# A transformer block on one core: the order of the beginning, before the first scores

## Chip, cores and metric

The kernel runs on one core of one Trainium2 chip. The metric is the device time of one execution in microseconds (us), the median over several runs. Lower is better.

## What is computed

The reference is one transformer block on x of shape 2 x 1024 x 256, with a context of shape 2 x 154 x 192, all in fp32: self-attention with 16 heads of 64, cross-attention to the context, and a gated feed-forward part. Cut to what matters:

```python
def _layernorm(x, g, b, eps=1e-05):
    mu = jnp.mean(x, axis=-1, keepdims=True)
    var = jnp.var(x, axis=-1, keepdims=True)
    return (x - mu) * jax.lax.rsqrt(var + eps) * g + b

h = _layernorm(x, ln1_g, ln1_b)
x = _attention(h, h, sa_wq, sa_wk, sa_wv, sa_wo, sa_bo) + x
h = _layernorm(x, ln2_g, ln2_b)
x = _attention(h, cond_emb, ca_wq, ca_wk, ca_wv, ca_wo, ca_bo) + x
h = _layernorm(x, ln3_g, ln3_b)
p = h @ ff_w1 + ff_b1
a, gate = (p[..., :D_FF], p[..., D_FF:])
h = a * jax.nn.gelu(gate, approximate=False) @ ff_w2 + ff_b2
return h + x
```

The change touches only the first layer norm of the first batch and the first three projection halves that read it.

## The kernel before

The order of all work is written out by hand: `tc.manual_schedule()` keeps every engine's instructions in the order in which the Python code issues them. There are three long loops, one for self-attention, one for cross-attention and one for the feed-forward part. In each step of a loop, some pieces of projections, norms and output products are run beside the attention work. A piece issues its TensorE work and returns a function, the store, which reads the result out of PSUM; `flush(stores)` calls the stores that are waiting.

Ahead of the first loop stands the beginning, which this case is about. Batch 0 of x is 8 tiles of 128 rows. They are loaded in four pairs (tiles 0-1, 2-3, 4-5, 6-7) by `load_x` at L79, pairs 0 and 4 by the queue of SP and pairs 2 and 6 by the queue of ACT (a pair is named by its first tile). The gain and shift of the first norm, the parameter columns `cols`, are loaded by the ACT queue at L94, one element per partition and row of 128, so in pieces of 4 bytes. The first weights and the other parameters follow on the queue of SP (L109, L133, L140, L104).

The norm has four kinds of pieces:

- `stats(t)` for one tile: the statistics `st_ln` (L190) and their aggregate `mv_ln` (L191), both on VectorE (DVE);
- `deviation(t)` for a pair: `var_ln` (L196, on DVE in the beginning) and `rstd_ln` by a power on GpSimd (POOL, L200);
- `normalize(t)` for a pair: the offset `off_ln` (DVE, L206) and two activations to `xn_ln` (ACT, L212);
- `turn(t)` for a pair: four TensorE (PE) transposes into a PSUM tile `ph_ln` (L221), and a store of two copies to `hT_ln`, one for each half c of the 256 features, with gain and shift applied. In the beginning both copies are on DVE (L230), elsewhere on ACT (L234).

`project_half` (L290) multiplies a weight slice with 512 rows of `hT_ln`: two products, for c = 0 and c = 1, of 512 columns each; the record holds two PE entries for each of them. The store is an ACT copy (L297 for keys, L298 for queries). The first half of rows is made of pairs 0 and 2, the second of pairs 4 and 6. The first scores (L370) need the queries of the first half (`q0`) and the keys of both halves (`k0`, `k1`).

Before the pieces, 26 transposes of the identity into an unused PSUM tile are run on PE (`warm`, L866). PSUM tiles come from `mm_tile` and `sum_tile`, pools of two banks each.

Of the kernel before, what the change touches and what calls it, by code (L numbers as in the profile page):

```python
# [13 lines left out]
P = 128  # L14
# [4 lines left out]
def tile_transformer_block(ctx: ExitStack, tc: tile.TileContext, a: dict, out: bass.AP):  # L19
    nc = tc.nc  # L20
    x, cond = a["x"], a["ctx_768"]
    w = {k[len("L0_xattn_"):]: v for k, v in a.items() if k.startswith("L0_xattn_")}
# [11 lines left out]
    NC = D // P  # L34
# [5 lines left out]
    HB = 512  # L40
# [23 lines left out]
    def mm_tile(name):  # L64
        return ps_m.tile([P, HB], F32, tag="mm", name=name)

    def sum_tile(name):

        return ps_o.tile([P, HB], F32, tag="po", name=name)
# [7 lines left out]
    def load_x(queue, b, t):  # L77

        queue.dma_start(  # L79
            out=xt[b, t // GT][:, t % GT:t % GT + 2, :],  # L80
            in_=x[b, t * P:(t + 2) * P, :].rearrange("(t p) d -> p t d", p=P),
        )
# [3 lines left out]
    names = ["ln1_g", "ln1_b", "ln2_g", "ln2_b", "ln3_g", "ln3_b", "ff_b1"]  # L86
    n_rows = sum(w[n].shape[0] // P for n in names)
    cols = const.tile([P, n_rows], F32, tag="cols", name="cols")
    row_of, r = {}, 0
    for n in names:  # L90
        k = w[n].shape[0] // P
        row_of[n] = r
        if n.startswith("ln1"):
            nc.scalar.dma_start(out=cols[:, r:r + k], in_=w[n].rearrange("(r p) -> p r", p=P))  # L94
            n_cols = r + k
        r += k
    rows = pp_.tile([n_rows - n_cols, P], F32, tag="P", name="rows")
    for t in range(0, NT, 2):
        load_x(nc.scalar if t % 4 else nc.sync, 0, t)
    bias = {}  # L100

    def load_bias(n):
# [13 lines left out]
    wsl, wo = {}, {}  # L116
# [14 lines left out]
    for n in names[2:]:  # L131
        k = w[n].shape[0] // P
        nc.sync.dma_start(  # L133
            out=rows[row_of[n] - n_cols:row_of[n] - n_cols + k, :],
            in_=w[n].rearrange("(r p) -> r p", p=P),
# [9 lines left out]
    ident = const.tile([P, P], F32, tag="ident", name="ident")  # L145
# [28 lines left out]
    def norm_pieces(kind, b, first=False):  # L174

        ln = {"sa": "ln1", "ca": "ln2", "ff": "ln3"}[kind]  # L180
        g0, b0 = row_of[ln + "_g"], row_of[ln + "_b"]
        st = {}

        def stats(t):
            if t == 0:
                st["hT"] = hT[kind, b] = p2.tile([P, NC, S], F32, tag="hT", name=f"hT_{ln}_{b}")
            if t % 2 == 0:
                st["mv", t] = small.tile([P, 2, 2], F32, tag="mv", name=f"mv_{ln}_{b}_{t}")
            s6 = small.tile([P, 6], F32, tag="st", name=f"st_{ln}_{b}_{t}")
            nc.vector.bn_stats(s6, xt[b, t // GT][:, t % GT, :])  # L190
            nc.vector.bn_aggr(st["mv", t // 2 * 2][:, t % 2, :], s6)  # L191

        def deviation(t):
            mv = st["mv", t]
            var = small.tile([P, 2], F32, tag="var", name=f"var_{ln}_{b}_{t}")
            (nc.vector if first else nc.gpsimd).tensor_scalar(  # L196
                var, mv[:, :, 1], EPS, 1.0, op0=ALU.add, op1=ALU.mult
            )
            rstd = small.tile([P, 2], F32, tag="rstd", name=f"rstd_{ln}_{b}_{t}")
            nc.gpsimd.tensor_tensor(rstd, var, power, ALU.pow)  # L200
            st["rstd", t] = rstd

        def normalize(t):
            rstd = st["rstd", t]
            off = small.tile([P, 2], F32, tag="off", name=f"off_{ln}_{b}_{t}")
            nc.vector.scalar_tensor_tensor(  # L206
                off, st["mv", t][:, :, 0], -1.0, rstd, op0=ALU.mult, op1=ALU.mult
            )
            pool, tag = (one, "xn") if narrow(kind, b) and not first else (pp_, "P")
            xn = st["xn", t] = pool.tile([P, 2, D], F32, tag=tag, name=f"xn_{ln}_{b}_{t}")  # L210
            for i in range(2):
                nc.scalar.activation(  # L212
                    xn[:, i, :], xt[b, t // GT][:, t % GT + i, :], AF.Identity,
                    bias=off[:, i:i + 1], scale=rstd[:, i:i + 1],
                )

        def turn(t):
            ph = spare["bank"](f"ph_{ln}_{b}_{t}").rearrange("p (c n) -> p c n", c=NC)
            for i in range(2):
                for c in range(NC):  # L220
                    nc.tensor.transpose(  # L221
                        ph[:, c, i * P:(i + 1) * P], st["xn", t][:, i, c * P:(c + 1) * P], ident
                    )

            def store():
                for c in range(NC):
                    own = st["hT"][:, c, t * P:(t + 2) * P]
                    gain, shift = cols[:, g0 + c:g0 + c + 1], cols[:, b0 + c:b0 + c + 1]
                    if first:
                        nc.vector.tensor_scalar(  # L230
                            own, ph[:, c, :], gain, shift, op0=ALU.mult, op1=ALU.add
                        )
                    else:
                        nc.scalar.activation(  # L234
                            own, ph[:, c, :], AF.Identity, bias=shift, scale=gain
                        )

            return store

        return (  # L240
            [lambda t=t: stats(t) for t in range(NT)],
            *([lambda t=t, f=f: f(t) for t in range(0, NT, 2)] for f in (deviation, normalize, turn)),
        )

    def narrow(kind, b):

        return kind == "sa" or kind == "ca" and b < B - 1
# [35 lines left out]
        side.append((False, (), lambda: add_biases(kind, b)))  # L283


    def project_half(dst, name, wt, h, n, mul=None):

        pq = mm_tile(f"p{name}_{n}")
        for c in range(NC):
            nc.tensor.matmul(  # L290
                pq, lhsT=wt[:, c, :], rhs=h[:, c, n * HB:(n + 1) * HB],
                start=(c == 0), stop=(c == NC - 1),
            )
        if mul is None:

            dk = dst.rearrange("p (h n j) -> p n h j", h=2, j=KB)[:, n * NK // 2:(n + 1) * NK // 2]
            return lambda: nc.scalar.copy(dk, pq.rearrange("p (n h j) -> p n h j", h=2, j=KB))  # L297
        return lambda: nc.scalar.activation(dst[:, n * HB:(n + 1) * HB], pq, AF.Copy, scale=mul)  # L298
# [20 lines left out]
    def self_pieces(b, pr):  # L319

        t = {}

        def start():
            t["h"] = hT["sa", b]
            t["q"] = p2.tile([P, S], F32, tag="QT", name=f"q_sa{b}_{pr}")
            t["k"] = p2.tile([P, S], F32, tag="KT", name=f"k_sa{b}_{pr}")
            t["v"] = pt_.tile([P, NT, 2, P], F32, tag="V", name=f"v_sa{b}_{pr}")
            qk["sa", b, pr] = (t["q"], t["k"], t["v"])

        def q(n):  # L330
            if n == 0:
                start()
            return project_half(t["q"], f"q_sa{b}_{pr}", wsl["sa", pr, "q"], t["h"], n, scale)

        def k(n):
            return project_half(t["k"], f"k_sa{b}_{pr}", wsl["sa", pr, "k"], t["h"], n)

        def v(n):
            return project_self_values(t["v"], wsl["sa", pr, "v"], t["h"], b, pr, n)

        return [lambda f=f, n=n: f(n) for f in (q, k, v) for n in range(2)]
# [88 lines left out]
    def run(piece):  # L430
        done = piece()
        if done is not None:
            (adds if getattr(done, "adds", False) else stores).append(done)

    def flush(queue):
        for fn in queue:
            fn()
        queue.clear()
# [142 lines left out]
    def cross_pieces(b, pr):  # L581
# [3 lines left out]
        def q(n):  # L585
            if n == 0:
                t["q"] = p2.tile([P, S], F32, tag="QT", name=f"q_ca{b}_{pr}")
                t["k"] = p2.tile([P, S], F32, tag="KT", name=f"k_ca{b}_{pr}")
                qk["ca", b, pr] = (t["q"], t["k"])
            return project_half(t["q"], f"q_ca{b}_{pr}", wsl["ca", pr, "q"], hT["ca", b], n, scale)  # L590
# [262 lines left out]
    with tc.manual_schedule():  # L853
        stats, deviation, normalize, turn = norm_pieces("sa", 0, True)
# [3 lines left out]
        def emit(*pieces):  # L858
            for piece in pieces:
                run(piece)  # L860
            flush(stores)


        warm = sum_tile("warm")
        for _ in range(26):
            nc.tensor.transpose(warm[:, :P], ident, ident)  # L866
        emit(stats[0], stats[1], deviation[0], stats[2], stats[3], deviation[1])
        emit(normalize[0], stats[4], stats[5], deviation[2])
        emit(normalize[1], turn[0])
        emit(normalize[2], turn[1])  # L870
        emit(stats[6], stats[7], deviation[3], q0, normalize[3], k0)
        emit(turn[2])
        emit(turn[3])
        emit(k1)
        later.append(lambda: load_pair("sa", units[1][1]))
        later.append(lambda: load_pair("sa", units[2][1]))
# [7 lines left out]
        for p in range(SA):  # L884
# [15 lines left out]
            h, hg = divmod(p, SH)  # L900
# [40 lines left out]
        for k in range(FF):  # L941
            c = CA + k
# [56 lines left out]
```

## Time and profile before

| What | Value |
|---|---|
| median of 3 runs | 1179.57 us (1178.59 to 1180.47) |
| the profiled execution, its own time | 1178.48 us |
| its span, first to last instruction | 1176.6 us |
| PE busy over the span | 1143.3 us, 97% |
| start of the first scores (L370) | 22.68 us |

The profile is of one execution. Times in it count from the first instruction, and the execution's own time is 1.9 us longer than its span. "PEclk" is the clock that TensorE was granted, 1.00 being full speed. The view of stages gives, for each stretch of time, each engine's busy time; the chain of waits follows the work back from the last instruction.

### The profile page before, as it was taken

What the parts mean: (1) busy time and instruction counts of PE and PEld (TensorE: products, weight loads), DVE (VectorE), ACT (ScalarE), POOL (GpSimd) and SP (SyncE); (2) the same over time, 40 slices, a digit from 0 to 9 for tenths busy, and PEclk for the clock granted to TensorE, in tenths of its full rate; (3) what the DMA queues carried; (4) which work ended last, traced back from release to release, by engine and by line L of the source; (5) the groups of instructions that cost most, each with busy time, mean ns of one, the idle gap of its engine ahead of it and who ended that gap; (6) DMA issues with size and microseconds to landing.
All of it is one profiled execution on the core that took longest, in us unless ns stands there. A gap on an engine that the chain in (4) does not pass through costs nothing.

```text
span 1176.6 us, 31689 instructions
## 1 busy us (share of the span) xinstructions
PE 1143.3 (97%) x11907; PEld 669.7 (57%) x11907; DVE 830.9 (71%) x1172; ACT 642.9 (55%) x2053; POOL 670.7 (57%) x1563
## 2 busy tenths in 40 slices
PE   7999999999999999999999988999999999999998
PEld 4434445545545545545545433665555567888887
DVE  3888888898888888889999888556655574232222
ACT  3656776666656656656666765456655572041111
POOL 1678777877777777777777777445644453030000
PEclk8999999999999999999999998999999999999999
DMA  2321011011111111111111110176444433000000
GB/s 63 92 61 27 18 27 21 22 33 21 26 25 22 24 25 21 28 22 21 28 23 21 24 21 6 46 173 156 102 107 102 102 80 73 1 19 9 18 10 18
DMA packets 87018, 51.06 MB, mean 43 GB/s; under 512 B 30742, under 2 KB 77650, under 8 KB 86866
## 3 DMA queue, kind: packets, MB, share of 16 engines
q1 hardware_dynamic: 83650, 46.42, 17.4%
q10 hardware_dynamic: 3216, 2.62, 0.7%
q8 instruction: 94, 1.54, 0.6%
q14 instruction: 58, 0.48, 0.1%
HBM read 19.52 MB, written 2.10 MB: 18 GB/s over the span
## 4 chain that ended last, share of the span: by engine, by line
PE 75%; POOL 6%; ACT 6%; DMA 4%; DVE 4%; issue 3%; SPq 2%; ACTq 0%; DVEq 0%; POOLq 0%
PE po L417 14%; PE s L370 13%; PE pa L809 9%; PE py_sa L348 5%; PE py_ca L348 5%; PE pf L832 5%; PE pq_ca L290 4%; ACT p L381 4%; PE poc L721 4%; DMA st<-st 3%; PE pk_sa L290 3%; PE pq_sa L290 3%; PE sc L645 3%; PE pv_sa L305 3%; POOL p L481 3%
## 5 line engine op out<-in xcount | busy, mean ns | idle before, releaser
L381 ACT ACTIVATE p<-s,st 128x512 f32<-128x512 f32 x512 | 345.2, 686 | 219.9 <-DVE st L530 210.4
L481 POOL TENSOR_SCALAR p<-p,rd,ee 128x512 f32<-128x512 f32 x512 | 387.6, 772 | 43.8 <-DVE rd L477 43.2
L530 DVE TENSOR_REDUCE st<-s 128x2 f32<-128x1024 f32 x256 | 301.4, 1219 | 45.9 <-PE s L370 38.1
L495 DVE STREAM_TRANSPOSE pT<-p 128x1024 f32<-128x1024 f32 x256 | 302.4, 1218 | 0.6 <-POOL p L481 0.5
L370 PE MATMUL s<-k_sa,q_sa 64*32 64x512 f32 x4096 | 256.4, 600 | 20.5 <-ACT p L381 19.3
L417 PE MATMUL po<-pT,v_sa 64*64 64x256 f32 x4096 | 236.3, 380 | 1.2 <-DVE pT L495 1.2
L417 PEld LDWEIGHTS po<-pT,v_sa 64*64 64x64 f32 x4096 | 151.0, 133 | 110.5 <-issue 40.4
L672 POOL TENSOR_SCALAR p<-p,rden 128x154 f32<-128x154 f32 x256 | 97.4, 402 | 119.3 <-DVE rden L669 118.1
L370 PEld LDWEIGHTS s<-k_sa,q_sa 64*32 64x32 f32 x4096 | 58.8, 106 | 153.8 <-ACT p L381 67.8
L661 ACT ACTIVATE p<-sc,neg 128x154 f32<-128x154 f32 x256 | 96.0, 394 | 88.6 <-DVE rden L669 84.4
L809 PE MATMUL pa<-hT_ln,wf 128*128 128x256 f32 x512 | 121.0, 379 | 0.0
L818 DVE SCALAR_TENSOR_TENSOR u<-pa,cols,gate 128x256 f32<-128x256 f32 x64 | 31.0, 484 | 124.1 <-ACT gate L815 124.1
L815 ACT ACTIVATE gate<-pa,cols 128x256 f32<-128x256 f32 x64 | 30.3, 474 | 152.1 <-PE pa L809 152.1
L809 PEld LDWEIGHTS pa<-hT_ln,wf 128*128 128x128 f32 x512 | 96.8, 190 | 13.7 <-issue 0.8
L381 ACT ACTIVATION_READ_ACCUMULATOR p<-s,st 128x1 f32 x512 | 103.5, 202 | 0.0
L650 DVE TENSOR_REDUCE neg<-sc 128x6 f32<-128x924 f32 (+1 forms) x48 | 48.6, 1013 | 48.3 <-PE sc L645 48.3
L405 POOL TENSOR_TENSOR zz<-ee,st 128x8 f32<-128x8 f32 x128 | 26.0, 203 | 84.3 <-ACT ee L403 84.3
L305 PEld LDWEIGHTS pv_sa<-sa_wv,hT_ln 128*128 128x128 f32 x512 | 59.3, 192 | 16.3 <-issue 12.9
L832 PE MATMUL pf<-wf,u 128*128 128x256 f32 x256 | 65.0, 379 | 0.2 <-DVE u L818 0.2
L305 PE MATMUL pv_sa<-sa_wv,hT_ln 128*128 128x128 f32 x512 | 62.4, 278 | 0.0
L290 PE MATMUL pq_sa<-hT_ln,sa_wq 128*128 128x512 f32 x128 | 61.2, 621 | 0.6 <-DVE hT_ln L230 0.6
L290 PE MATMUL pk_sa<-hT_ln,sa_wk 128*128 128x512 f32 x128 | 60.7, 610 | 1.2 <-DVE hT_ln L230 1.2
(73 smaller groups left out, 1228.4 us busy)
## 6 DMA issues: line engine op xcount, KB each, us to landing
wf<-pT_ca SPq DMA_DIRECT2D x128, 128.0 KB
st<-st SPq DMA_DIRECT2D x512, 1.0 KB
v_sa<-v_sa SPq DMA_DIRECT2D x64, 128.0 KB
wf<-in_L_xattn_ff_w_dram SPq DMA_DIRECT2D x12, 256.0 KB
sa_wq<-in_L_xattn_sa_wq_dram SPq DMA_DIRECT2D x16, 128.0 KB
sa_wk<-in_L_xattn_sa_wk_dram SPq DMA_DIRECT2D x16, 128.0 KB
sa_wv<-in_L_xattn_sa_wv_dram SPq DMA_DIRECT2D x16, 128.0 KB
ca_wq<-in_L_xattn_ca_wq_dram SPq DMA_DIRECT2D x16, 128.0 KB
```

What stands on the lines that cost most here:

```text
L290: nc.tensor.matmul(pq, lhsT=wt[:, c, :], rhs=h[:, c, n * HB:(n + 1) * HB], start=(c == 0), stop=(c == NC - 1),)
L305: nc.tensor.matmul(pv[:, i * P:(i + 1) * P], lhsT=h[:, c, (n * GT + i) * P:(n * GT + i + 1) * P], rhs=wt[:, c, :], start=(c == 0), stop=(c ...
L348: nc.tensor.matmul(py[:, :D], lhsT=o[:, i, t * P:(t + 1) * P], rhs=wo[kind][:, half * HP + i, :], start=(i == 0), stop=(i == HP - 1),)
L370: nc.tensor.matmul(sc[a4 * KB:(a4 + 1) * KB, j, :], lhsT=q[r, c:c + KB], rhs=k[r, h * HB:(h + 1) * HB], start=True, stop=True, tile_positi ...
L381: nc.scalar.activation(pr[:, j, :], sc[:, j, :], AF.Exp, bias=st[:, 0, 0, i, j:j + 1], accum_out=st[:, 0, 1, i, j:j + 1],)
L417: nc.tensor.matmul(po[a2][j * DH:(j + 1) * DH, :QH // 2], lhsT=v[r, t, e, j * DH:(j + 1) * DH], rhs=pT[r, j * NK + n, :], start=(t == 0 an ...
L481: nc.gpsimd.tensor_scalar(pr[:, j, :], pr[:, j, :], rd[:, c:c + 1], ee[:, 0, c:c + 1], op0=ALU.mult, op1=ALU.mult,)
L495: nc.vector.transpose(halves[h][:, :, c:c + KB], groups.pop(0).rearrange("p j (n k) -> p (j n) k", k=KB))
L530: nc.vector.tensor_reduce(st[:, 0, 0, i, :], sc[i], AX.X, ALU.max, negate=True)
L672: nc.gpsimd.tensor_scalar(pr_[:, j, i, :T], pr_[:, j, i, :T], rden[:, j, i:i + 1], 1.0, op0=ALU.mult, op1=ALU.mult,)
L809: nc.tensor.matmul(pa[:, half, :TF * P], lhsT=w1[:, c, half * DF + f * P:half * DF + (f + 1) * P], rhs=h[:, c, t0 * P:(t0 + TF) * P], star ...
L832: nc.tensor.matmul(sums[blk][i][:, :D], lhsT=sums[blk, "u"][:, f, i * P:(i + 1) * P], rhs=w2[:, f, :], start=(f == 0), stop=(f == NF - 1),)
```

## The change

Five edits, all in the beginning:

1. The two loads of `cols` are issued behind the loads of x on the ACT queue, not ahead of them.
2. The pieces are emitted in another order: `deviation` and `normalize` of pair 0 come earlier among the statistics, `turn(4)` stands between `q0` and `k0` on PE, and `turn(6)` between `k0` and `k1`. Before, both stood behind `k0`.
3. The copies of pairs 2 and 6 are shared: c = 0 stays on DVE and c = 1 goes to ACT.
4. The identity transposes become 46: 32 at the start, 10 behind the transposes of pair 0 and 4 behind those of pair 2. They use a tile of the other PSUM pool.
5. `k1` is computed in two parts of 256 columns, so that the first part needs only pair 4.

```diff
         row_of[n] = r
         if n.startswith("ln1"):
-            nc.scalar.dma_start(out=cols[:, r:r + k], in_=w[n].rearrange("(r p) -> p r", p=P))
             n_cols = r + k
         r += k
     rows = pp_.tile([n_rows - n_cols, P], F32, tag="P", name="rows")
     for t in range(0, NT, 2):
         load_x(nc.scalar if t % 4 else nc.sync, 0, t)
+    for n in names[:2]:
+        k = w[n].shape[0] // P
+        nc.scalar.dma_start(
+            out=cols[:, row_of[n]:row_of[n] + k], in_=w[n].rearrange("(r p) -> p r", p=P)
+        )
...
-                    if first:
+                    if first and (c == 0 or t % 4 == 0):
                         nc.vector.tensor_scalar(
                             own, ph[:, c, :], gain, shift, op0=ALU.mult, op1=ALU.add
                         )
...
-    def project_half(dst, name, wt, h, n, mul=None):
+    def project_half(dst, name, wt, h, n, mul=None, parts=1):
 
         pq = mm_tile(f"p{name}_{n}")
-        for c in range(NC):
-            nc.tensor.matmul(
-                pq, lhsT=wt[:, c, :], rhs=h[:, c, n * HB:(n + 1) * HB],
-                start=(c == 0), stop=(c == NC - 1),
-            )
+        for i in range(parts):
+            own = slice(i * HB // parts, (i + 1) * HB // parts)
+            for c in range(NC):
+                nc.tensor.matmul(
+                    pq[:, own], lhsT=wt[:, c, :],
+                    rhs=h[:, c, n * HB + own.start:n * HB + own.stop],
+                    start=(c == 0), stop=(c == NC - 1),
+                )
...
         def k(n):
-            return project_half(t["k"], f"k_sa{b}_{pr}", wsl["sa", pr, "k"], t["h"], n)
+            parts = 2 if (b, pr, n) == (0, 0, 1) else 1
+            return project_half(
+                t["k"], f"k_sa{b}_{pr}", wsl["sa", pr, "k"], t["h"], n, parts=parts)
...
-        warm = sum_tile("warm")
-        for _ in range(26):
-            nc.tensor.transpose(warm[:, :P], ident, ident)
-        emit(stats[0], stats[1], deviation[0], stats[2], stats[3], deviation[1])
-        emit(normalize[0], stats[4], stats[5], deviation[2])
-        emit(normalize[1], turn[0])
-        emit(normalize[2], turn[1])
-        emit(stats[6], stats[7], deviation[3], q0, normalize[3], k0)
-        emit(turn[2])
-        emit(turn[3])
+        warm = mm_tile("warm")
+
+        def busy(n):
+            for _ in range(n):
+                nc.tensor.transpose(warm[:, :P], ident, ident)
+
+        busy(32)
+        emit(stats[0], stats[1], deviation[0])
+        emit(stats[2], normalize[0], stats[3], deviation[1])
+        copies = turn[0]()
+        busy(10)
+        emit(stats[4], normalize[1])
+        copies()
+        emit(stats[5], deviation[2])
+        copies = turn[1]()
+        busy(4)
+        copies()
+        emit(normalize[2], stats[6], stats[7], deviation[3])
+        q_copy, copies = q0(), turn[2]()
+        emit(normalize[3])
+        q_copy()
+        copies()
+        k_copy, copies = k0(), turn[3]()
+        k_copy()
+        copies()
         emit(k1)
```

In the lists `normalize`, `deviation` and `turn` an index counts pairs, so `turn[2]` is the `turn` of pair 4; in `stats` it counts tiles. The loops behind `emit(k1)` are the same in both kernels.

## The prediction

> **What bounds the kernel now.** I read the totals first: PE is busy 97% of the span, and behind 22.68 us the loops are the same in both kernels. Nothing in them waits for a moment of absolute time, so the change is worth what it moves the start of the first scores (L370). The chain of waits for the beginning says what leads there. Its columns are start, duration, and what.
>
> ```profile
> 0.72 0.48 ACTq L94
> 1.24 0.51 ACTq L94
> 1.77 5.43 DMA x<-in_x_dram
> 7.23 0.44 DVE st_ln L190
> ...
> 10.05 0.61 ACT xn_ln L212
> 10.70 1.20 PE ph_ln L221 x4
> 11.92 0.56 DVE hT_ln L230
> 12.52 3.75 PE pq_sa L290 x4
> 16.27 1.72 PE pk_sa L290 x4
> 17.98 0.45 PE ph_ln L221 x4
> 18.46 1.46 DVE hT_ln L230 x3
> 20.05 1.97 PE pk_sa L290 x4
> 22.04 0.59 ACT k_sa L297
> 22.68 1.17 PE s L370 x16
> ```
>
> First comes pair 2 of x, on the ACT queue behind the two column loads, landing at 7.2. Then DVE does the statistics in order, then come xn, the transposes, the copies and q0. The query product takes 3.75 us; the key product of the same size behind it takes 1.72. The view of stages says why (columns: length, PE, PEld, DVE, ACT, POOL busy, PEclk, DMA share, GB/s):
>
> ```profile
> 1.38:6.60 5.22, 5.22 (x26) 4.98 (x26) 1.27 (x5) 1.28 (x1) 0.71 (x1) 1.00 0.82 207
> 6.60:9.35 2.75, 0.00 (x1) 0.00 (x0) 1.98 (x9) 0.65 (x2) 0.67 (x1) 0.99 0.48 138
> 9.35:12.52 3.17, 2.36 (x8) 1.16 (x9) 2.25 (x9) 2.38 (x5) 0.72 (x2) 0.50 0.39 115
> 12.52:16.28 3.76, 3.76 (x5) 1.69 (x6) 1.73 (x7) 1.19 (x3) 0.69 (x1) 0.52 0.00 0
> 16.28:22.68 6.40, 4.53 (x16) 2.01 (x15) 1.90 (x4) 1.79 (x4) 0.00 (x0) 1.00 0.00 0
> ```
>
> PE idles 2.75 us behind the identity transposes, then its clock is 0.50 until the end of the query product. In the last stage it is busy only 4.53 of 6.40: the transposes of pairs 4 and 6 come together behind k0, and k1 waits for four DVE copies in a row.
>
> [...] asked by half microseconds, the clock falls near 9.25 and returns near 16.08[...]: 0.76 of 3.41 us (5.84 to 9.25) lost the clock, 2.17 (19.49 to 22.9) kept it. [...] with both queues full the trace shows 372 and 361 GB/s (5.5 to 6.5 us), with SP's alone 177 to 187 (2.5 to 4.5). [...]
>
> **The change, part by part.**
>
> *Columns behind x.* The SP loads keep their order. On ACT, pair 2 is issued at 0.72 in place of 1.77. Each column load costs 0.5 us of issue on ACT, which has nothing to run until 4.35, so the issue is free in both places. Pair 0 landed at 4.30 with 256 KB at about 185 GB/s. With both queues full the sum was 360, so pair 2 can land at 4.3 to 4.5 without delaying pair 0; the bad end is both at 5.7, were 185 the limit of both together. Pairs 4 and 6 follow at about 5.7, before DVE wants them. The columns now run last. Before, the ACT queue's four loads were through by about 7.6; the same four in another order should also end near 7.6, plus 0.7 for the landing: 8.3. [...] (sa_wv waited 1.7 us for the gain column). Its row, context and bias loads may now wait for the columns, some 2 us more. They are wanted from 23 us on, so this is covered; without cover those 2 us would count.
>
> *DVE order.* From the rows of DVE a statistics/aggregate pair costs 0.53, var 0.17, off 0.15; rstd on POOL 0.7 (5.76 to 6.47). Tiles 0 and 1 and var end at 5.68 as before. Tile 2 fits in while POOL works, off of pair 0 comes at 6.50 (was 8.51). xn of pair 0 is 6.69 to 7.79 (two of 0.59, overlapping), its transposes 7.34 to 8.2. Its copies wait for the columns: 8.3 to 9.29. Tile 3, var, tile 4 and off of pair 2 (8.20) stand ahead of these copies, so xn of pair 2 runs 8.39 to 9.49 whatever the columns do. Behind the copies stand tile 5 and var of pair 4, to 10.04.
>
> *Identity transposes.* At full clock one costs 0.13 us (8 of pairs 4 and 6 in 1.04). The first 26 took 5.22 us, 0.20 each, though the stage shows 1.00: I read them as half clock, 0.21 each, up to about 5.8, where the last ones come faster. 32 end near 7.0 in the profiled phase, ahead of xn; 8.2 in the worst, which costs 0.6. The 10 fill 8.1 to 9.4 and make pair 2 some 0.3 late: its transposes end at 10.0. The 4 lie behind them while the copies run: no cost. PE is busy about 2.9 of 3.41 us from 5.84 to 9.25 and 3.0 in the next window, above the 2.17 that kept the clock. So q0 should run in 1.9 us, as k1 did, and not 3.75.
>
> *Shared copies.* Two DVE copies take 0.99; one on each engine ends after 0.58 (the ACT copy of L234 averages 579 ns). Pair 2 is ready at 10.62 and q0 runs 10.62 to 12.52, against 12.52 to 16.27.
>
> *Pairs between projections.* On DVE, off of pair 4 follows the copy of pair 2 at 10.84, xn is 11.03 to 12.12, and tiles 6 and 7 end with var at 12.26. Its transposes follow q0, 12.5 to 13.0, and k0 13.03 to 14.9. rstd and off of pair 6 end at 13.22, xn 13.25 to 14.34. The query copy is queued behind xn on ACT and slips to 14.84; k1's bank waits for it, but only from 15.45. The copies of pair 4 (13.2 to 14.2, DVE) lie beside k0. The key copy runs 14.95 to 15.54. The transposes of pair 6 run 14.9 to 15.45, copies to 16.13, beside the first part of k1 (15.45 to 16.3). The second part ends at 17.2, its copy at 17.84, scores start at **17.9**.
>
> *The sum.* 22.68 - 17.9 = 4.8 us: 1.9 from q0's clock, about 1.9 from q0's earlier start, the rest (1.0) behind q0. The profiled execution would become 1178.5 - 4.8 = 1173.7. It stands 1.1 below the median of the runs; [...] I keep the same gain: 1179.6 - 4.8 = **1174.8**. Unknowns: pair 2 late costs up to 1.4; a worst phase 0.6; on the other side, executions whose half clock now lasts longer than in the profile would gain up to about 2 more. So this case by itself spans 1172.5 to 1176.8.
>
> **Rivals.**
>
> *The clock falls again* (chance 0.15). If pair 2 comes late (5.7), PE idles beyond 2 us behind its 32 transposes, a window falls to about half busy, between the 0.76 us that lost the clock and the 2.17 that kept it. Then the 10 transposes cost 2.1 instead of 1.3 and q0 its 3.75: 4.8 - 0.8 - 1.9 = 2.1 gained, **1177.5**. For it: the gap between transposes and xn remains. Against: at 4.4 the gap is only some 0.4 us.
>
> *The early load brings nothing* (0.08). If x is no earlier, since the SP transfers take the engines, q0 starts as before and stays at half clock; only the copies and pairs behind q0 count: about 1.0 and 0.4 from pair 2, 1.4 in all, **1178.2**. Against: ACT's x packets reached 0.15 MB in half a microsecond beside SP's.
>
> *The columns land late and take the clock with them* (0.05; the slower one). Every copy needs them, and DVE is in order, so behind pair 0's copies all of tile 5, var and pair 2's copy wait. ACT's shared copy waits too, with xn of pair 4 behind it. From 8.3 on a microsecond late is a microsecond lost; PE has nothing of its own beyond 10.5. At 10 us the gap before q0 is nearly 2 us and the half clock threatens q0, k0 and half of k1 (1.9 + 1.8 + 0.9 = 4.6). From a landing at 11.0 this decides: 2.7 of wait and 4.6 of clock against 4.8 gained, 2.5 slower, **1182.1**. For it: 512 packets of 4 bytes took from 2.5 to 5.5 us. Against: the whole ACT queue took until 7.6 with the same content.
>
> That the later loops give the gain back has no anchor in the trace[...].
>
> **How the numbers follow.** The likeliest case has 0.72: 1174.8. A measurement of this kernel can tell 0.2%, 2.4 us, from no change: faster is below 1177.2, slower above 1181.9. Of the first case 0.70 lies below, of the second 0.06, of the third, by scatter, 0.02: faster has 0.78. Late columns leave 0.04 for slower, and the remaining 0.18 is the same. For eight in ten the range runs from 1172.4 to 1177.7, into the second case.
>
> **What would show it.** Right: off of pair 0 near 6.5; PEclk 1.00 from 6 to 20 us; the first L290 group of 1.9 us; scores from 17.9. Wrong: DVE waiting at the copies of pair 0 for columns beyond 8.5; statistics of tile 2 waiting for x beyond 5.6; PEclk 0.50 at q0; an earlier first score without an earlier end.

## The result, and the profile after

The changed kernel takes 1172.25 us (1171.99 to 1172.41, 5 runs) against 1179.57 before; the ratio is 0.9942, with a 95% interval of 0.9931 to 0.9954. So it is 7.3 us faster, where 4.8 was forecast. Two later sets gave 1172.90 against 1179.13 and 1172.73 against 1179.38: 6.2 and 6.7 us. The profiled execution took 1171.99 us with a span of 1170.1, 6.5 us less than before, and its scores start at 17.41 us, 5.3 earlier.

The chain of waits of the changed kernel, as shown for the kernel before (start, duration, what):

```profile
1.38 5.94 PE warm L877 x32
7.32 0.56 PE ph_ln L225 x4
7.93 0.99 DVE hT_ln L234 x2
8.92 0.34 DVE st_ln L194
...
9.68 0.50 DVE hT_ln L234
10.23 1.98 PE pq_sa L296 x4
12.21 0.44 PE ph_ln L225 x4
12.65 1.72 PE pk_sa L296 x4
14.37 0.44 PE ph_ln L225 x4
14.80 1.95 PE pk_sa L296 x8
16.78 0.59 ACT k_sa L304
17.41 1.17 PE s L379 x16
```

The landing of x no longer stands in it as a piece of its own; the identity transposes do, since the last of them end at 7.32, behind the first of the two activations that write xn of pair 0 (6.28 to 6.87). From 10.23 to 16.75 PE goes from one product to the next, with the two transposes between them, and the query product takes 1.98 us in place of 3.75. The same stretches as before in the view of stages (PE, PEld, DVE, ACT, POOL busy, PEclk, DMA share, GB/s):

```profile
6.60:9.35 2.75, 2.75 (x25) 2.41 (x24) 2.37 (x9) 1.86 (x4) 0.69 (x1) 1.00 0.19 42
9.35:12.52 3.17, 2.97 (x15) 1.72 (x15) 2.13 (x9) 1.56 (x3) 1.20 (x2) 1.00 0.29 95
12.52:16.28 3.76, 3.76 (x17) 2.28 (x16) 1.61 (x4) 2.61 (x5) 0.18 (x1) 1.00 0.00 0
```

PEclk is 1.00 in all three, where it was 0.99, 0.50 and 0.52.

### The profile page after: what moved, and what is told of

It reads as the page before. It is cut to its first block, busy times and chain, and to the rows that moved or that the text cites. A ratio compares the mean times of both kernels' runs of the same rounds, so it can differ in the third digit from the quotient of the medians.

```text
span 1170.1 us, 31736 instructions
## 1 busy us (share of the span) xinstructions
PE 1142.5 (98%) x11931; PEld 672.0 (57%) x11931; DVE 830.1 (71%) x1170; ACT 644.1 (55%) x2055; POOL 667.5 (57%) x1563
## 4 chain that ended last, share of the span: by engine, by line
PE 78%; ACT 7%; POOL 6%; DVE 3%; issue 3%; DMA 2%; SPq 1%; DVEq 0%; ACTq 0%; POOLq 0%
PE po L426 15%; PE s L379 15%; PE pa L818 9%; PE py_sa L357 5%; PE py_ca L357 5%; PE pf L841 5%; ACT p L390 4%; PE pq_ca L296 4%; PE poc L730 4%; PE pv_sa L312 4%; PE pk_sa L296 3%; POOL p L490 3%; PE pq_sa L296 3%; PE sc L654 3%; DMA st<-st 2%
## 5 line engine op out<-in xcount | busy, mean ns | idle before, releaser
L379 PE MATMUL s<-k_sa,q_sa 64*32 64x512 f32 x4096 | 256.7, 601 | 19.1 <-ACT p L390 18.0
L296 PE MATMUL pk_sa<-hT_ln,sa_wk 128*128 128x512 f32 (+1 forms) x132 | 60.8, 596 | 0.2 <-ACT q_sa L305 0.2
L357 PE MATMUL py_ca<-ca_wo,o_ca 128*128 128x256 f32 x256 | 60.8, 384 | 0.3 <-ACT hT_ln L238 0.3
```

Of the source, the lines that this page charges most:

```text
L296: nc.tensor.matmul(pq[:, own], lhsT=wt[:, c, :], rhs=h[:, c, n * HB + own.start:n * HB + own.stop], start=(c == 0), stop=(c == NC - 1),)
L357: nc.tensor.matmul(py[:, :D], lhsT=o[:, i, t * P:(t + 1) * P], rhs=wo[kind][:, half * HP + i, :], start=(i == 0), stop=(i == HP - 1),)
L379: nc.tensor.matmul(sc[a4 * KB:(a4 + 1) * KB, j, :], lhsT=q[r, c:c + KB], rhs=k[r, h * HB:(h + 1) * HB], start=True, stop=True, tile_positi ...
```

## The experiments

Twelve further runs were made: of eight other kernels, and of the two kernels again, each twice. The table gives one profile of each run: the time of off of pair 0, the distances from there to q0, from q0 to k0 and from k0 to the scores, the start of the scores, and the rest of the span behind it; the last column is the median of the runs.

| Kernel | off | to q0 | to k0 | to scores | scores | rest | median |
|---|---|---|---|---|---|---|---|
| before | 8.51 | 4.01 | 3.57 | 6.59 | 22.68 | 1153.9 | 1179.57 |
| before, again | 8.63 | 4.00 | 3.58 | 6.60 | 22.81 | 1154.9 | 1 run |
| before, a third time | 8.80 | 4.01 | 3.28 | 6.58 | 22.68 | 1154.7 | 1 run |
| columns behind x alone | 6.89 | 3.76 | 3.23 | 6.86 | 20.75 | 1154.1 | 1176.92 |
| filling alone | 8.63 | 4.44 | 2.42 | 6.58 | 22.07 | 1152.7 | 1175.81 |
| changed | 6.08 | 4.15 | 2.26 | 4.93 | 17.41 | 1152.7 | 1172.25 |
| changed, again | 6.72 | 4.14 | 2.26 | 4.93 | 18.05 | 1152.9 | 1172.90 |
| changed, a third time | 6.16 | 4.14 | 2.26 | 4.93 | 17.50 | 1154.7 | 1172.73 |
| less filling | 6.61 | 4.22 | 4.43 | 5.66 | 20.92 | 1152.8 | 1175.64 |
| columns first | 7.81 | 4.11 | 2.26 | 4.93 | 19.10 | 1150.6 | 1173.17 |
| all copies on DVE | 6.32 | 4.14 | 2.26 | 4.92 | 17.64 | 1153.5 | 1172.95 |
| k1 whole | 6.54 | 4.14 | 2.26 | 5.68 | 18.62 | 1152.9 | 1174.22 |
| pairs behind k0 | 6.65 | 4.14 | 1.82 | 5.83 | 18.45 | 1152.4 | 1172.13 |
| further edits | 5.73 | 4.48 | 2.26 | 4.19 | 16.66 | 1154.1 | 1171.83 |

The last row is not to be compared by its scores: there a part of them starts before k1 is ready. Its first row maximum (L546) is compared instead. The runs belong to four sets, and the kernel before was measured in each: its median was 1179.57 beside the first run of the changed kernel, 1178.61 beside the four from columns behind x to columns first, 1179.13 beside the changed kernel's second run and the three that undo one edit more (copies, k1, pairs), and 1179.38 beside its third run and the further edits. Gains in the median are taken within a set, and compared between sets by the ratio to the kernel before.

### One part alone, or one undone: columns and clock

**Columns behind x, alone.** To the kernel before:

```diff
-            nc.scalar.dma_start(out=cols[:, r:r + k], ...)
...
     for t in range(0, NT, 2):
         load_x(nc.scalar if t % 4 else nc.sync, 0, t)
+    for n in names[:2]:
+        nc.scalar.dma_start(out=cols[:, ...], ...)
```

> The kernel before with the first edit alone: columns loaded behind x on the ACT queue. Theory 1 (the gain is early x plus a held clock, and early x brings much of the clock by closing PE's idle gap): off of pair 0 near 6.5 us in place of 8.5; scores start at 18.7 if the clock holds through q0, at 20.6 if it is lost near 9.3. Theory 2 (the order of pieces is what counts, x alone is hidden by DVE's order): scores start no earlier than 21.5. The end moves with the start of the scores in both; if the rest of the span (end less start of scores, 1153.9 us before and 1152.7 after) differs from 1153.9 by more than 1 us, that part has its own scatter.

Measured: off of pair 0 at 6.89, so the pair is early, and scores at 20.75. The clock was lost: PEclk is 0.50 from 11.03 to 14.45. The view of stages, in stretches of 3.41 us, called windows here: in the profile of the kernel before, PEclk changes at 9.27, 16.10, 715.83, 719.25, 729.49 and 732.90, so 2, 205, 1, 3 and 1 times 3.413 us apart.

```profile
4.20:7.62 3.42, 1.59 (x14) 1.35 (x13) 3.04 (x14) 1.82 (x3) 1.26 (x2) 1.00 0.87 239
7.62:11.03 3.41, 2.13 (x9) 1.10 (x10) 2.75 (x10) 2.74 (x6) 0.83 (x2) 1.00 0.35 108
11.03:14.45 3.42, 3.42 (x5) 1.35 (x4) 1.36 (x7) 0.98 (x2) 0.69 (x1) 0.50 0.01 2
```

In the window from 7.62 PE was busy 2.13 of 3.41 us, PEclk was 0.50 in the next one, and q0 took 3.44 us. In the window from 4.20 it was busy only 1.59 us, and PEclk stayed at 1.00; the last section comes back to this. Theory 1 in its lost-clock form holds; theory 2 (21.5 or later) falls. The median gained 1.7, against 1.9 in the start.

**Filling, alone.** To the kernel before, with the tile of the other PSUM pool as in the change:

```diff
-        for _ in range(26):
+        busy(46)
...
         emit(normalize[1], turn[0])
+        busy(4)
         emit(normalize[2], turn[1])
+        busy(6)
```

> The kernel before with identity transposes alone added: 46 at the start (to about 9.3 us), 4 behind those of pair 0 and 6 behind those of pair 2, everything else as before. Theory 1: the clock stays at 1.00 from 6 us on, q0 takes 1.9 us in place of 3.75, but the transposes of pair 6 then wait for xn, so scores start at 21.2, a gain of 1.5; the executions also scatter less than the 1.9 us of the kernel before (1178.6 to 1180.5)[...]. Theory 2: the clock is not what q0's length hangs on, or the later pieces eat the gain: scores at 22.4 or later, scatter as before.

Measured: scores at 22.07, neither. In this execution the 46 transposes took 6.61 us and were over at 8.0, and PE idled 1.5 us before pair 0:

```profile
7.65:11.06 3.41, 1.88 (x14) 1.14 (x11) 2.89 (x14) 1.99 (x4) 1.38 (x2) 1.00 0.35 102
11.06:14.47 3.41, 3.41 (x12) 2.44 (x11) 2.62 (x9) 1.29 (x3) 0.08 (x1) 0.50 0.06 20
```

So filling with a fixed number of transposes did not hold the clock here, with x late: 1.88 us busy, then PEclk 0.50. The scatter did not shrink either (1173.75 to 1177.31), against theory 1. The median gained 2.8, though the start of this profile gained only 0.6: its rest is short, 1152.7, and how the clock stood in the other executions is not on record.

**The changed kernel with less filling.**

```diff
-        busy(32)
+        busy(26)
...
-        busy(10)
...
-        busy(4)
```

> The changed kernel with 26 identity transposes at the start and none later (as many as before). Theory 1 (the filling holds the clock): a window of 3.41 us is about 2 us busy, near the 2.17 that kept the clock before; if it is lost at 9.4, q0 and k0 take 3.75 and more, and scores start near 21 in place of 17.4, and executions scatter by 2 us or more. Theory 2 (early x already closes the gap, the filling is idle ornament): clock 1.00 throughout, scores at 17.2, since PE is free 0.2 us earlier for pair 0.

Measured: scores at 20.92, executions from 1172.88 to 1176.27, the median 0.9963 of the kernel before, where the changed kernel has 0.9942 to 0.9945: 2.1 to 2.5 us slower. Both marks of theory 1. The stages by windows:

```profile
6.49:9.90 3.41, 1.96 (x12) 0.99 (x10) 2.89 (x11) 2.18 (x4) 0.78 (x2) 1.00 0.39 104
9.90:13.32 3.42, 2.78 (x5) 1.18 (x4) 2.22 (x10) 1.54 (x3) 1.38 (x2) 0.50 0.21 31
13.32:16.73 3.41, 3.41 (x8) 1.76 (x7) 1.09 (x3) 1.69 (x3) 0.00 (x0) 0.50 0.00 0
```

PEclk is 0.50 behind 1.96 us busy, and still 0.50 behind 2.78 of 3.42 at half clock. Behind the full window k1 takes 2.10 us, as in the changed kernel at PEclk 1.00. From q0 to the scores it takes 10.09 us against 7.18: a loss of 2.9, enough for the whole of the median's difference.

**The changed kernel with the columns first.** The first diff, undone.

> The changed kernel with the column loads ahead of x again. Theory 1: pair 2 lands at 7.2, off of pair 0 moves from 6.1 to 7.9, scores from 17.4 to 19.1 with the clock held, to 21 or later if the gap between the 32 transposes and pair 0 loses it. Theory 2: the new order hides the late pair, since only one of its tiles stands ahead of off of pair 0: scores at 17.9 at most.

Measured: off at 7.81 and scores at 19.10, the 19.1 of theory 1; behind off everything is as in the changed kernel (11.30 us to the scores against 11.33). PEclk stayed at 1.00, behind a window less busy than those of the changed kernel ahead of q0 (3.41 us in its first profile, 3.20 in its third):

```profile
7.08:10.50 3.42, 2.60 (x22) 2.12 (x21) 2.85 (x11) 1.90 (x4) 0.69 (x1) 1.00 0.45 132
```

So this much filling held the clock even with the pair late by 1.1 to 1.7 us. By these ratios, 0.9947 against 0.9942 to 0.9945, the median lost 0.6 or less against these 1.1 to 1.7 in the start, and this profile even ended earlier than the changed one, since its rest is the shortest of all.

### The other edits

**All copies on DVE.**

```diff
-                    if first and (c == 0 or t % 4 == 0):
+                    if first:
```

> The changed kernel with all eight copies of hT on DVE again. As I forecast it (the two copies of a pair run side by side, 0.4 us saved for pairs 2 and 6): scores start about 0.5 later, at 17.9. By the profile of the changed kernel (the ACT copy started only when the DVE copy of the same pair had ended, 10.21 after 10.17 and 15.42 after 15.38): sharing saves nothing, and scores start at 17.3, 0.1 earlier, since a second DVE copy follows the first with 0.45 of pitch.

Measured: the distance from off to the scores is 11.32 us against 11.33, so neither the 0.5 nor the 0.1 came. The timeline of DVE in this kernel, and after it those of DVE and of ACT in the changed one (start, duration, what, idle before):

```profile
9.87 1.00 DVE L234 TENSOR_SCALAR hT_ln<-ph_ln,cols 128x256 f32<-128x256 f32 x2
```

```profile
9.63 0.54 DVE L234 TENSOR_SCALAR hT_ln<-ph_ln,cols 128x256 f32<-128x256 f32 x1
...
14.84 0.54 DVE L234 TENSOR_SCALAR hT_ln<-ph_ln,cols 128x256 f32<-128x256 f32 x1 [1.04 <-PE ph_ln L225]
```

```profile
10.21 0.56 ACT L238 ACTIVATE hT_ln<-ph_ln,cols 128x256 f32<-128x256 f32 x1 [1.11 <-DVE hT_ln L234]
...
15.42 0.57 ACT L238 ACTIVATE hT_ln<-ph_ln,cols 128x256 f32<-128x256 f32 x1 [0.40 <-DVE hT_ln L234]
```

The last bracket names what ended ACT's wait: the DVE copy of the same pair. Two copies take 1.00 on DVE and 0.54 + 0.04 + 0.56 = 1.14 shared. Sharing brought nothing; it cost nothing either, since the copy for c = 1 is wanted only when the product for c = 0 is over. ACT's copy starts 0.04 us behind the end of DVE's. Why it waits is not shown: both copies read one PSUM tile, `ph_ln`, and write one tile, `hT_ln`, and neither two PSUM tiles nor two `hT_ln` tiles were tried.

**k1 in one part.**

```diff
-            parts = 2 if (b, pr, n) == (0, 0, 1) else 1
+            parts = 1
```

> The changed kernel with k1 in one part of 512 columns. If the split lets half of k1 run beside the copies of pair 6: the first product can start only at 15.4 and the second only when ACT's copy ends at 16.0, so k1 ends near 17.2 in place of 16.75 and scores start at 17.85, 0.45 later. Rival (k1 waits for its PSUM bank or the last copy anyway): scores at 17.4 to 17.5.

Measured: 0.75 us more from off to the scores, where 0.45 was expected. Its chain of waits:

```profile
15.30 0.55 DVE hT_ln L234
15.99 1.97 PE pk_sa L296 x4
17.98 0.59 ACT k_sa L304
18.62 1.17 PE s L379 x16
```

All of k1 now stands behind the DVE copy of pair 6. The split is worth 0.75 in this profile.

**Pairs 4 and 6 behind k0.**

```diff
-        q_copy, copies = q0(), turn[2]()
...
+        emit(q0, normalize[3], k0)
+        emit(turn[2])
+        emit(turn[3])
```

> The changed kernel with the transposes of pairs 4 and 6 together behind k0, as before; all else as changed. If standing between the projections is worth something: the copies of both pairs then follow k0 in a row (three on DVE, one on ACT), from 14.6 to 16.7, part one of k1 waits to 15.6, scores start near 18.1, 0.7 later. Rival (PE has the same work in any order and xn of pair 6 comes at 14.1 anyway): scores at 17.4 to 17.6.

Measured: 0.47 us more (11.80 against 11.33); 0.7 was expected. Its chain:

```profile
14.64 0.48 ACT q_sa L305
15.12 0.48 ACT k_sa L304
15.66 2.12 PE pk_sa L296 x8
17.81 0.59 ACT k_sa L304
18.45 1.17 PE s L379 x16
```

The chain puts k1's start down to ACT's key copy, over at 15.60. The first DVE copy of pair 4 ends at 15.51, so late that the two can't be told apart here; the product itself takes 2.12 in place of 1.95. The median, 1172.13, is not above the changed kernel's beside it, 1172.90: half a microsecond in the start does not show there.

**Further edits**, to look for a better version:

```diff
+    for t in range(GT):
+        (nc.scalar if t % 2 else nc.sync).dma_start(
+            out=xt[0, 0][:, t, :], in_=x[0, t * P:(t + 1) * P, :]
+        )
-    for t in range(0, NT, 2):
+    for t in range(GT, NT, 2):
...
-        busy(32)
+        busy(27)
...
+        parts = 2 if u == "0_0" else 1
+        for i in range(parts):
...
-                    rhs=k[r, h * HB:(h + 1) * HB], start=True, stop=True,
+                        rhs=k[r, h * HB + own.start:h * HB + own.stop], start=True, stop=True,
```

> The changed kernel with three further edits: pairs 0 and 2 loaded tile by tile over both queues, 27 identity transposes at the start in place of 32 so that they end before the earlier xn, and the first score tile computed in two halves of 256 columns, the first of which needs only k0 and runs beside k1's copy. If the landing of pair 0 is what the beginning hangs on: off of pair 0 near 5.6 (6.1 to 6.7 in the changed kernel), the rest of the chain the same 11.3 us to the end of k1's copy, and the first row maximum 0.6 nearer to it: 1.0 to 1.3 us gained at the first row maximum, end near 1171.5. Rival (two loads in flight share the rate, or the columns now land later and hold the copies): the first row maximum within 0.6 us of the changed kernel's. In both, the scatter of the later loops, about a microsecond, may hide it in the median.

Measured: the first row maximum at 18.17 us, against 18.61, 19.25 and 18.69 in the changed kernel, so 0.4 to 1.1 gained; against the changed kernel beside it (18.69) it is 0.5, which is the rival's side. Which of the three edits brought it was not tried apart. Its chain:

```profile
7.47 0.42 DMA rows<-in_L_xattn_ln_b_dram
...
7.96 0.99 DVE hT_ln L238 x2
...
16.76 0.59 ACT k_sa L308
17.40 0.75 PE s L386 x16
18.17 1.24 DVE st L546
```

Off of pair 0 is early (5.73), but now the copies wait for a load until 7.9. The profile names it by its source, the shifts of the norms; of the loads from there, these copies read only the shift column: q0 comes 4.48 behind off in place of 4.14. The earlier x and the late column both count. The median is 1171.83, the lowest of all, but its runs (1170.90 to 1173.24) overlap those of the changed kernel beside it (1170.71 to 1174.12): no difference that can be told.

**Both kernels unchanged, again.**

> The changed kernel once more, for its scatter and another phase of the clock windows. If the filling holds the clock in every phase, scores start within 0.5 us of 17.4 and PEclk stays 1.00 up to the end of self-attention; executions lie within 1 us of each other. If the tight first runs (1172.0 to 1172.4) were one lucky phase, scatter is 2 us and scores may start at 19 or later. The rest of the span (1152.7 in the first profile) may differ by a microsecond either way if that part scatters by itself.

> The changed kernel once more beside the further edits, on the same chip. Scores start 11.3 us behind off of pair 0, as in both profiles of it; the start itself within 17.4 to 18.1, by the landing of x. Were the clock lost before the scores in this phase, they would start 11.3 plus 2 or more behind it.

> The kernel before once more, for another phase of the clock windows. If the phase decides how long its clock stays halved: q0 takes 1.9 to 3.75 and k0 1.9 to 3.75, so scores start anywhere from 21 to 24 us, and the distance from off of pair 0 to the scores differs from the 14.2 of the first profile. If the halved stretch is set by the program: 14.2 again.

> The kernel before a further time, as the run above: another draw of the phase. Distance from off of pair 0 to the scores 14.2 again if the program sets the halved stretch, 12.5 to 16 if the phase does.

Measured: the changed kernel has 11.33 us from off to the scores in all three profiles; from q0 to k0 it has 2.26 us each time, where half clock gave 4.43 with less filling. Its windows lie differently: one begins at 5.98 in the first profile, at 5.03 in the third. What varies is when pair 0 lands (first statistics at 3.88, 4.52 and 3.96). Its executions are not always as close as in the first set: 1170.7 to 1174.5 later. Three forecasts for the second run missed: scores came at 18.05, not within 0.5 of 17.4; the executions spread over 2.0 us, not 1; and the clock was lost for one window within self-attention, at 74.5 us (the mean granted over the span was 0.995, against 0.997 in the first profile). The kernel before has 14.17, 14.18 and 13.87, and from q0 to k0 3.57, 3.58 and 3.28: too much alike to say what another phase would do to it.

## Why the prediction was right, and what it mis-sized

The direction and the mechanism hold: early x, held clock, pairs between projections. Point by point, from 22.68 to 17.41 us:

- **Early pair 0.** Forecast: off at 6.50. Measured 6.08 here, 6.72 and 6.16 in the other two. The step said that pair 0 would land as before, at 4.30; it landed between 3.88 and 4.52, by chance more than by the change (4.25 to 4.34 in the kernel before), so 0.4 of the 2.4 us gained here in the first profile is luck. The order on DVE did what was worked out: off is 2.20 us behind the first statistics, 4.21 before. With early x and the old order it is 2.55, with the new order and late x 3.35: most of this part is early x.
- **Columns.** Forecast landing 8.3. They were there by 7.93 in the changed kernel and were waited for until 7.9 in the last experiment, so the estimate was about 0.4 too late. The row and context loads, which were to wait some 2 us more, did not: the context load was issued at 7.87, before at 8.36. (The load `sa_wv` is SP's fifth; it waited 1.7 us for the gain column before and 1.4 us for x in the changed kernel.) The slower rival did not come true, and with off so early, neither did the one in which the early load brings nothing.
- **The clock.** Forecast 1.9 for q0; it fell from 3.75 to 1.98, 1.8. With less filling, the half clock reaches k0 too and costs 2.9. The rival in which the clock falls again is real, then, but only with the filling gone: early x alone did not hold the clock (0.50 from 11.03 to 14.45), which the prediction left open. The two busy times that it compares with (0.76 us ahead of half clock, 2.17 ahead of full) do not make a rule: in columns behind x alone PEclk was 0.50 behind 2.13 and 1.00 behind 1.59. The 32 transposes were to end near 7.0; from its own figures (26 over at 6.60, 0.13 for each more) 7.4 follows, and they ended at 7.32. That cost nothing: in the third profile they are over at 6.86, and off to q0 takes the same 4.14.
- **Shared copies.** This step failed: it had the two engines side by side, 0.58 for 0.99. They run in turn, 1.14 for both, and undoing the edit changed 0.01 us. The start of q0 still came out right, since only the c = 0 copy decides it.
- **Behind q0.** Forecast about 1.0. Measured 0.75 for the split and 0.47 for the order, 1.2; from q0 to the scores 7.18 us, forecast 7.28. One reading was off: k1 of the kernel before waited for three DVE copies, as the chain has it (`x3`), not four.

These add up: 2.4 (off) - 0.1 (off to q0) + 1.8 (clock) + 1.2 = 5.3.

**The term that was mis-sized** is the last one, "I keep the same gain". The first median, 1172.25, lies just below the range given for eight in ten (1172.4 to 1177.7), the later two, 1172.90 and 1172.73, just inside it. Over three profiles of each the scores start 5.07 us earlier on average (22.72 to 17.65), while the medians differ by 6.2 to 7.3. One to two microseconds come from behind the first scores. I had named half-clock stretches of other lengths in the kernel before, with no trace behind it; over its three profiles the distance from off to the scores differs by 0.3 us at most. The rest of the span was 1153.9 to 1154.9 before and 1152.7 to 1154.7 after: lower on average by 1.0, but all profiles of this study, with loops that are the same, lie between 1150.6 and 1154.9 without order by the start (the shortest rest goes with scores at 19.10, and scores at 17.41 and 17.50 go with 1152.7 and 1154.7). So the rest has a scatter of some 4 us of its own, and whether the change has a hand in the missing microsecond is open. The traces show where it arises. The row maxima follow each other in the same order in all these kernels; counted from the first of them, the three profiles of the kernel before are on average 1.0 us later than the three of the changed one after 301 us already, and no more at the last. So it arises in the first 300 us of the loops. What varies there is how long PE waits for the softmax before it may run the next scores: in these 300 us 10.8, 12.1 and 10.5 us in all in the kernel before, 10.2, 8.7 and 11.5 in the changed one, 1.0 less on average, and 9.2 in the profile with the shortest rest. What sets these waits is not shown, and with such scatter three profiles of each do not show a difference between the kernels. That a shift of the beginning arrives at the end one for one is true only within this scatter.

## What to carry to other kernels

Look at the beginning of a kernel as a chain with its own clock: here a short idle stretch ahead of the first real products cost more than the stretch itself. With less filling, 1.45 us of idle PE from 6.49 to 9.90 were followed by PEclk 0.50, and the scores came 2.9 us later behind q0. Bring the data earlier and fill what is left: here each of the two alone lost the clock. Undo each part of a bundle and measure from one fixed event to the next: here early x, the filling, the split of k1 and the place of pairs 4 and 6 counted, the shared copies did not, and differences of 0.5 us were clear in those distances and invisible in the median. Two copies out of one PSUM tile ran one behind the other here, 1.14 us for both, although they sat on two engines: look at the timeline before counting them as parallel.

## What the runs showed of the hardware

- The steps of 3.413 us that lie between changes of PEclk in the kernel before are found in the changed kernel too: PEclk is 0.50 from 709.13 to 712.54 and from 722.78 to 726.20, and 722.78 lies 4 times 3.413 us behind 709.13.
- How busy PE was in a window, and PEclk in the next one. For the first profiles of the two kernels these are, but for the end of the span, all windows at full clock behind which PEclk fell, and the least busy one of each behind which it did not; the other rows are from the views above.

| Run | Window | PE busy | PEclk in the next |
|---|---|---|---|
| before | 5.86 to 9.27 | 0.74 | 0.50 |
| before | 726.07 to 729.49 | 0.99 | 0.50 |
| changed | 719.37 to 722.78 | 1.03 | 0.50 |
| before | 712.42 to 715.83 | 1.09 | 0.50 |
| changed | 705.72 to 709.13 | 1.11 | 0.50 |
| columns behind x alone | 4.20 to 7.62 | 1.59 | 1.00 |
| before | 74.13 to 77.54 | 1.77 | 1.00 |
| changed | 70.84 to 74.25 | 1.86 | 1.00 |
| filling alone | 7.65 to 11.06 | 1.88 | 0.50 |
| less filling | 6.49 to 9.90 | 1.96 | 0.50 |
| columns behind x alone | 7.62 to 11.03 | 2.13 | 0.50 |
| columns first | 7.08 to 10.50 | 2.60 | 1.00 |

- Between 1.59 and 2.13 us both happened, so busy time, as the profile models it, does not settle it alone there. The three windows of 1.88, 1.96 and 2.13 consist mostly of transposes, and the record of those includes short waits: four of one pair take 0.93 us with the wait for the second half of xn, eight in a row 1.04. Counted at 0.13 each, the window with 2.13 held some 1.4 us of work (an estimate: 8 x 0.13, and 0.38 of q0), less than the 1.59 that kept the clock.
- At half clock, PEclk was still 0.50 behind windows with 2.53 us busy (the kernel before, 9.27 to 12.69) and 2.78 (less filling, 9.90 to 13.32). It was 1.00 behind 3.24 and 3.29 (the kernel before, from 729.49 and 715.83) and behind 3.41 (its window from 12.69).
- PEclk reads 1.00 from the start of the kernel before, but its identity transposes are recorded with 421 ns each from 2.0 to 5.5 us and with 273 from 5.9 to 6.6. The same 26 took 4.42 us in columns behind x alone, 5.22 in the kernel before and 5.53 with less filling.
- With x on both queues from the start, the landing of the same 256 KB still varied from 3.88 to 4.52 us.
